# Six diffusion layers: attention outputs in four tiles of 32 columns, and values only for the heads that a half of the partitions keeps

## The chip, the cores and the metric

The kernel runs on one core of a Trainium2 chip. Its time is the device time of one execution in microseconds (us). A profiled execution gives the span, from the first to the last recorded instruction, and the duration of every instruction on every engine: TensorE (PE, with its weight loads listed apart as PEld), VectorE (DVE), ScalarE (ACT), GpSimd (POOL) and the DMA queue of SyncE (SP).

## What is computed

The program is a chain of eight residual blocks on x of 16 batches x 64 tokens x 128 features: a recurrent decoder, a mixture of experts, a latent attention, a quantised feed-forward, then the block of this case, then another mixture, an attention block and a last mixture. The block of this case has six layers, each with 16 heads of 8 features:

```python
for i in range(NL):                                   # NL = 6
    xn = _adaln(x, noise_emb, n1_w[i], n1_b[i])
    q, k, v = jnp.split(xn @ qkv_w[i].T, 3, axis=-1)
    q, k = _rope(q), _rope(k)
    x = x + _attn(q, k, v, src_mask).reshape(B, L, D) @ so_w[i].T
    xn = _adaln(x, noise_emb, n2_w[i], n2_b[i])
    q, k, v = _rope(xn @ cq_w[i].T), _rope(context @ ck_w[i].T), context @ cv_w[i].T
    x = x + _attn(q, k, v, ctx_mask).reshape(B, L, D) @ co_w[i].T
    xn = _adaln(x, noise_emb, n3_w[i], n3_b[i])
    x = x + gelu(xn @ f1_w[i].T + f1_b[i]) @ f2_w[i].T + f2_b[i]
```

`_attn` is a masked softmax over 64 keys; `_adaln` is a layer norm with a scale and a shift per batch; `_rope` is a rotary embedding. All arithmetic is in fp32.

## The kernel before

The six layers are written by `layers` (L2087). Every layer works on two halves of the batches, h = 0 and 1, of 8 batches (512 tokens) each, and in each half it does self attention ("s"), cross attention ("c") and a feed-forward. The keys and values of cross attention depend only on the context and are computed for a whole layer at its head.

The order of the work is not written by hand. Every step is put down with `plan.op(engine, ns, emit, deps, takes, ...)`: the engine it runs on, an assumed duration in ns, what it depends on, and the kind of buffer that it takes. `_Plan.order` (L1183) then goes through the steps greedily: of all steps that are ready, the one that could start first goes next, and of those that could start together the one with the longest remaining path. The instructions of each engine are emitted in that order, and each engine keeps it. So an assumed duration has no effect on what an instruction costs, but it sets the order of all instructions of the stage. `_Plan.fills` (L1234) adds small bf16 matmuls (`units`) to the PE queue where the plan leaves PE idle or sees little activity (from each step's `area`); they compute nothing that is used.

Buffers in PSUM are few: two of kind `pj` (one bank each, for projections and transposes), one `S` (four banks, scores) and one `O` (two banks, attention outputs). A step that takes a buffer waits until the one who had it before has been read out.

**One attention of one half** (`attend_half`, L2354). After the norm and two projections for queries (`rotary_half`), `qx` holds queries of which all but 8 of each 32 partitions are zeroed, so that one matmul with 32 rows gives the scores of one head per group of partitions. The partitions of a score tile are 64 keys for each of two heads: the lower 64 partitions belong to one head of a pair, the upper 64 to the other. Then, for each p of four (two batches each):

- `scores`: 16 fp32 matmuls into S (the trace has 32 weight loads and 32 matmuls of it, two for each);
- P = exp(S) by ACT, 128 x 1024 (L2405);
- `outputs`: 16 fp32 matmuls, each with a weight tile of P of 128 partitions x 64 columns (64 queries) and 18 moving columns of V: 16 with the values of a pair of heads, and two that give the softmax's sums.

For two p together, `inv` is the reciprocal of the sums (L2414) and `On` the normalised output (L2418), both on DVE; then a transpose (L2424), a copy by ACT (L2426), the output projection, and the addition to x (L2431).

**Keys and values** (`keys_values`, L2329). V is a tile of 128 partitions x (8 batches, 8 pairs of heads, 18). On the lower 64 partitions only the first head's 8 values of each pair may be non-zero, on the upper 64 only the second's, since both are summed over all partitions. The kernel before computes all 128 value features on both halves of the partitions (two matmuls for each batch, one for each half of the partitions, 128 moving columns), four batches to a `pj` buffer, so two buffers for a half. DVE multiplies by `pk`, the product of the key mask and of `par`, which is zero where a partition's half does not keep the head:

```python
nc.vector.tensor_tensor(V[:, g * 4:(g + 1) * 4, :, 0:16], t.slot[1]...,
    pk.unsqueeze(2).to_broadcast([128, 4, 8, 16]), ALU.mult)
```

Every value of V is thus written anew for every layer, except columns 16 and 17 of each pair, which are set once by two POOL instructions for each of the six V tiles (L2130; one tile for each half of self attention, two for each half of cross attention).

The decoder, at the start of the program, uses another tiling of TensorE in `mm4` (L1334): a product with 128 output partitions is cut into four matmuls of 32 weight columns. Its steps `su` and `cb` have 16 and 2 moving columns. It is not touched by the change.

Of the kernel before, what the change touches and what calls it, by code (L numbers as in the profile page):

```python
# [14 lines left out]
ALU = mybir.AluOpType  # L15
# [3 lines left out]
B, T, D = 16, 64, 128  # L19
# [1269 lines left out]
class _Fast(_Net):  # L1289
# [797 lines left out]
    def layers(self):  # L2087
        nc, tc = self.nc, self.tc
        x0 = self.x
        out = self.new_x()  # L2090
        with ExitStack() as st:
            pool = st.enter_context(tc.tile_pool(name="l_sb", bufs=1))
            ps = st.enter_context(tc.tile_pool(name="l_ps", bufs=1, space=PSUM))
            plan = _Plan()

            buffers = self.plan_buffers(plan, pool)
            buffers("pj", 2, [128, 512], where=ps)
            buffers("S", 1, [128, 4, 512], where=ps)
            buffers("O", 1, [128, 2, 512], where=ps)
            at = self.at["l"]  # L2100
            for (kind, a, b), n in zip(self.LPARTS, (2, 1, 1, 2, 1)):
                buffers(kind, n, [128, at[b][1] - at[a][0]], True)
            for kind, n, shape in (
                *self.NORM, ("xT", 3, [128, 512]), ("u", 3, [128, 2, 512]), ("qr", 2, [128, 512]),
                ("qx", 2, [128, 2048]), ("On", 4, [128, 2, D]), ("oT", 4, [128, 256]),
                ("ada", 2, [128, 6, B]),
                ("P", 8, [128, 1024]),
            ):
                buffers(kind, n, shape, kind == "ada")
            self.plan, self.inv = plan, self.tile(pool, [128, NL, 2, 2, 64], "inv")  # L2110


            self.keep = []
            for k, n in (("s", 1), ("c", 2)):
                u8 = pool.tile([128, B], U8, tag="u8" + k, name="u8" + k)
                nc.sync.dma_start(out=u8, in_=self.ins["km_" + k])
                m8 = self.tile(pool, [128, B], "m8" + k)
                nc.vector.tensor_copy(m8, u8)
                nc.vector.tensor_scalar(m8, m8, -1.0, 1.0, ALU.mult, ALU.add)
                pk = self.tile(pool, [128, B, 16], "pk" + k)  # L2120
                nc.vector.tensor_tensor(
                    pk, self.c("par").unsqueeze(1).to_broadcast([128, B, 16]),
                    m8.unsqueeze(2).to_broadcast([128, B, 16]), ALU.mult)
                self.keep.append(pk)
                for h in range(2):
                    buffers(f"kr{k}{h}", n, [128, 512], True)
                    vs = [self.tile(pool, [128, 8, 8, 18], f"V{k}{h}{v}") for v in range(n)]
                    for V in vs:
                        for c in range(2):
                            nc.gpsimd.tensor_tensor(  # L2130
                                V[:, :, :, 16 + c], self.c("par2")[:, c:c + 1].unsqueeze(1).to_broadcast([128, 8, 8]),
                                m8[:, h * 8:(h + 1) * 8].unsqueeze(2).to_broadcast([128, 8, 8]), ALU.mult)
                    plan.buffers(f"V{k}{h}", vs, True)
            ctxT = self.tile(pool, [128, NTOK], "ctxT")

            def context(h):
                t = plan.op("PE", 900, lambda t: [nc.tensor.transpose(
                    t[:, k * 128:(k + 1) * 128], self.ctx[:, h * 4 + k, :], self.ident) for k in range(4)], (), "pj", area=427)
                return plan.op("ACT", 600, lambda _: nc.scalar.copy(ctxT[:, h * 512:(h + 1) * 512], t.slot[1]), [t])

            cs = [context(h) for h in range(2)]
            xs = [out[:, h * 4:(h + 1) * 4, :] for h in range(2)]

            qs = [[self.quarter_norm(x0[:, h * 4:(h + 1) * 4, :], k, None, True, xs[h]) for k in range(2)]
                  for h in range(2)]
            tops = [[o for _, o in qs[h]] for h in range(2)]
            for n in range(NL):
                w = self.layer_loads(n)
                kv = [self.keys_values(w, "c", cs[h], lambda h=h: ctxT[:, h * 512:(h + 1) * 512], h) for h in range(2)]
                ada = self.layer_adapt(w)  # L2150
                for h in range(2):
                    tops[h] = self.attend_half(w, "s", n, h, xs[h], ada, None, tops[h],
                                               [q for q, _ in qs[h]] if n == 0 else None)
                for h in range(2):
                    tops[h] = self.attend_half(w, "c", n, h, xs[h], ada, kv[h], tops[h])
                for h in range(2):
                    tops[h] = self.ffn_half(w, h, xs[h], ada, tops[h], x0 if n == NL - 1 else None)
            with tc.manual_schedule(engines=None):
                plan.run(fill=self.fill, banks=("pj", "S", "O"))
            self.watch(0, self.inv.rearrange("p n k h t -> p (n k h t)"))  # L2160
        self.x = out
# [167 lines left out]
    def keys_values(self, w, kind, dep, src, h):  # L2329


        nc, plan = self.nc, self.plan
        c = "" if kind == "s" else "c"
        V = plan.op("SP", 0, lambda _: None, takes=f"V{kind}{h}")
        kr = self.rotary_half(w, (c + "k", c + "ks"), src, dep, f"kr{kind}{h}", [V])
        load, wv = w(c + "v")
        Vs = []
        for g in range(2):

            def values(t, g=g):  # L2340
                for k in range(4):
                    bt = (g * 4 + k) * T
                    keys = src()[:, bt:bt + T]
                    for r in (slice(0, 64), slice(64, 128)):
                        self.mm(t[r, k * 128:(k + 1) * 128], keys, wv())

            t = plan.op("PE", 1050, values, [load, dep], "pj", peers=[V])
            pk = self.keep["sc".index(kind)][:, h * 8 + g * 4:h * 8 + g * 4 + 4, :]
            Vs.append(plan.op("DVE", 690, lambda V, g=g, t=t, pk=pk: nc.vector.tensor_tensor(
                V[:, g * 4:(g + 1) * 4, :, 0:16], t.slot[1].rearrange("p (b c v) -> p b c v", b=4, c=8),  # L2350
                pk.unsqueeze(2).to_broadcast([128, 4, 8, 16]), ALU.mult), [t], on=V))
        return kr, Vs

    def attend_half(self, w, kind, n, h, x, ada, kv, top, ns=None):  # L2354

        nc, plan = self.nc, self.plan
        i = "sc".index(kind)
        c = "" if kind == "s" else "c"
        xT = self.adaln_half(x, ada, i, h, top, ns)
        src = lambda: xT[0].home.slot[1]  # L2360
        qr = self.rotary_half(w, (c + "q", c + "qs"), src, xT, "qr")
        kr, Vs = self.keys_values(w, kind, xT, src, h) if kv is None else kv
# [3 lines left out]
        def copy(t, j):  # L2366
# [5 lines left out]
            else:  # L2372
# [3 lines left out]
        qxs = [plan.op("ACT" if j == 3 else "DVE", 730 if j == 3 else 450, lambda t, j=j: copy(t, j), [qr], on=qx,  # L2376
                       peers=[qx]) for j in (3, 0, 1, 2)]
        O = plan.op("SP", 0, lambda _: None, [kr] + qxs, "O")

        def scores(S, p):  # L2380
            for bb in range(2):
                b = 2 * p + bb
                tok = slice(b * T, (b + 1) * T)
                for h2 in range(2):
                    for g in range(4):
                        rows = slice(32 * g, 32 * g + 32)
                        at = (b * 2 + h2) * 128
                        self.mm(S[h2 * 64:(h2 + 1) * 64, g, bb * 128:(bb + 1) * 128],
                                kr.slot[1][rows, tok], qx.slot[1][rows, at:at + 128])

        def outputs(O, p, P):
            Pv = P.slot[1].rearrange("p (g b q t) -> p g b q t", g=4, b=2, q=2)
            for g in range(4):
                for q in range(2):
                    for bb in range(2):
                        hp = 2 * g + q
                        at = (p % 2) * 144 + hp * 18
                        self.mm(O[bb * 64:(bb + 1) * 64, p // 2, at:at + 18], Pv[:, g, bb, q, :],
                                Vs[0].home.slot[1][:, 2 * p + bb, hp, :])

        load, wo = w(c + "o")
        os, adds = [], []
        for p in range(4):
            S = plan.op("PE", 950, lambda S, p=p: scores(S, p), [kr] + qxs, "S", peers=[O], area=427)
            P = plan.op("ACT", 1030, lambda P, S=S: nc.scalar.activation(  # L2405
                P.rearrange("p (g c) -> p g c", g=4), S.slot[1][:, :, 0:256], AF.Exp,
                scale=1.0 / math.sqrt(8.0)), [S], "P", table="exp")
            os.append(plan.op("PE", 950, lambda O, p=p, P=P: outputs(O, p, P), [P, *Vs], on=O, area=240))
            if p % 2 == 0:
                continue  # L2410
            k = p // 2
# [122 lines left out]
```

## Time and profile before

| | |
|---|---|
| three runs | 1675.52, 1684.32, 1690.44 us; median 1684.32 |
| the profiled execution | 1676.6 us, of which the span is 1672.9 |
| stage of the six layers | about 603 to 1176 us of the span |
| one layer in the middle | 797.8 to 890.0 us: 92.2 us |
| PE busy in that layer | 81.0 us; DVE 60.2, ACT 34.9, POOL 21.6 |
| O matmuls in that layer | 512 matmul records in 16 steps, 17.4 us busy |
| value matmuls in that layer | 128 records in 8 groups of 16, 8.4 us busy |
| scores in that layer | 512 records in 16 steps; P by ACT 16 x 1020 ns |
| granted PE clock in that layer | 1.00 |

A matmul's record is longer than the distance to the next one, since matmuls overlap: 32 records of about 212 ns stand within 1.1 us. The price of a step of many matmuls is therefore taken from the start of its first record to the start of what follows it on PE.

### The profile page before, as it was taken

To read this page: it belongs to the slowest core of one execution; us is meant where nothing else is said; L and a number is where in the kernel's file an instruction comes from. 1 tells how busy PE (TensorE), PEld (TensorE's weight loads), DVE (VectorE), ACT (ScalarE), POOL (GpSimd) and SP (SyncE) were. 2 spreads that over 40 slices of the span, in tenths; PEclk is the share of its full clock that TensorE was granted. 3 is DMA by queue.
4 is the path that set the end of the run, shared out by engine and by line. 5 is a ranking of instruction groups with operands and counts; after the bars stand their busy time and mean duration, and the time that the engine had idled before them with its cause. 6 is when DMAs were issued, how large, how long until landed. Compare 5 with 4: busy or idle time off the path is not lost.

```text
span 1672.9 us, 47624 instructions
## 1 busy us (share of the span) xinstructions
PE 1501.6 (90%) x21466; PEld 1092.4 (65%) x21466; DVE 783.3 (47%) x2505; ACT 536.1 (32%) x885; POOL 185.5 (11%) x227
## 2 busy tenths in 40 slices
PE   6999989999997599998898888888999899999997
PEld 5888856666777246666565656655576677776665
DVE  4435351226334656556676667565311544445112
ACT  2111134432331213424343333434433233332431
POOL 0000010002000032222222122122000101001000
PEclk7555579999999769989999999999999999999999
DMA  6000000000000041000000000000300200000000
GB/s 223 4 5 4 4 2 1 0 1 2 1 2 10 0 175 30 7 25 18 29 17 20 13 20 12 7 16 2 140 2 1 102 2 2 3 2 1 1 1 15
DMA packets 14338, 38.48 MB, mean 23 GB/s; under 512 B 1682, under 2 KB 6674, under 8 KB 14125
## 3 DMA queue, kind: packets, MB, share of 16 engines
q1 hardware_dynamic: 14125, 35.34, 6.2%
q8 instruction: 170, 2.79, 0.7%
q14 instruction: 43, 0.35, 0.1%
HBM read 34.81 MB, written 0.52 MB: 21 GB/s over the span
## 4 chain that ended last, share of the span: by engine, by line
PE 82%; DVE 12%; ACT 3%; issue 2%; DMA 1%; SPq 0%; POOL 0%; ACTq 0%; DVEq 0%
PE pj L296 41%; PE y L296 11%; PE O L296 9%; PE S L296 6%; PE cb L296 3%; PE hh L296 3%; PE lg L296 3%; DVE qx L2373 2%; DVE u L2323 1%; PE pj L1928 1%; ACT P L2451 1%; PE su L296 1%; PE pj L2264 1%; ACT bd L1568 1%; DVE nq L2211 1%
## 5 line engine op out<-in xcount | busy, mean ns | idle before, releaser
L296 PEld LDWEIGHTS y<-m_sb,H 128*128 128x128 f32 x1568 | 188.6, 192 | 57.3 <-issue 35.6
L296 PE MATMUL y<-m_sb,H 128*128 128x128 f32 x1568 | 193.5, 276 | 16.8 <-DVE x L1732 9.8
L296 PE MATMUL pj<-xT,m_sb 128*128 128x512 f32 x392 | 183.8, 598 | 0.0
L2217 POOL TENSOR_TENSOR nq<-nq,minus_half 128x2 f32<-128x2 f32 x120 | 85.2, 715 | 602.1 <-DVE nq L2214 568.5
L2405 ACT ACTIVATE P<-S 128x1024 f32<-128x1024 f32 x96 | 97.9, 1020 | 111.3 <-PE S L296 111.3
L1708 ACT ACTIVATE H<-pj,m_sb 128x512 f32<-128x512 f32 x128 | 87.5, 687 | 132.7 <-PE pj L296 132.4
L1732 DVE SCALAR_TENSOR_TENSOR x<-y,cw,x 128x128 f32<-128x128 f32 x128 | 39.0, 346 | 186.8 <-PE y L296 186.8
L296 PEld LDWEIGHTS pj<-xT,m_sb 128*128 128x128 f32 x392 | 68.9, 191 | 57.4 <-issue 56.9
L2247 ACT ACTIVATE xn<-x,nq 128x128 f32<-128x128 f32 x100 | 48.4, 492 | 152.4 <-DVE nq L2220 142.6
L2323 DVE TENSOR_TENSOR u<-pj,consts_sb 128x512 f32<-128x512 f32 x96 | 66.2, 690 | 35.4 <-PE pj L296 35.0
L1838 DVE COPY QKV<-pj 128x512 f32<-128x512 f32 x56 | 38.7, 691 | 72.5 <-PE pj L296 72.3
L296 PE MATMUL cb<-bd,E 128*32 128x2 f32 x4096 | 65.5, 193 | 3.3 <-issue 3.2
L1708 ACT ACTIVATE H<-pj,b1g,m_sb 128x512 f32<-128x512 f32 x64 | 49.6, 778 | 58.5 <-PE pj L296 55.8
L296 PEld LDWEIGHTS cb<-bd,E 128*32 128x32 f32 x4096 | 62.9, 156 | 3.5 <-issue 3.3
L296 PE MATMUL pj<-xT,w_sb 128*128 128x512 f32 x128 | 63.0, 611 | 1.4 <-DVE xT L2292 1.4
L296 PE MATMUL pj<-xT,l_f 128*128 128x512 f32 x96 | 50.4, 618 | 11.9 <-ACT P L2451 11.8
L1895 ACT ACTIVATE P<-S 128x1024 f32<-128x1024 f32 x32 | 32.8, 1024 | 85.0 <-PE S L296 84.7
L1732 DVE SCALAR_TENSOR_TENSOR acc<-y,cw,acc 128x128 f32<-128x128 f32 x64 | 19.5, 346 | 86.5 <-PE y L296 86.5
L296 PE MATMUL pj<-units 128*128 128x512 bf16 x195 | 55.7, 396 | 4.5 <-DVE x L2079 1.9
L1584 ACT ACTIVATE H<-hh 128x16 f32<-128x16 f32 x64 | 12.9, 202 | 138.8 <-PE hh L296 138.8
L296 PEld LDWEIGHTS O<-QKV,P 64*64 64x64 f32 (+1 forms) x1536 | 48.7, 135 | 13.2 <-issue 5.3
L296 PE MATMUL O<-QKV,P 64*64 64x65 f32 (+1 forms) x1536 | 55.2, 222 | 2.0 <-DVE On L1923 1.8
(363 smaller groups left out, 2738.9 us busy)
## 6 DMA issues: line engine op xcount, KB each, us to landing
w_sb<-in_w SPq DMA_DIRECT2D x7, 681.5 KB, 8.3
m_sb<-in_m SPq DMA_DIRECT2D x8, 515.0 KB, 7.6
m_sb<-in_m SPq DMA_DIRECT2D x8, 514.5 KB, 5.9
m_sb<-in_m SPq DMA_DIRECT2D x7, 565.5 KB, 9.3
l_f<-in_l SPq DMA_DIRECT2D x6, 578.5 KB, 3.9
l_a<-in_l SPq DMA_DIRECT2D x6, 387.0 KB, 3.1
l_s<-in_l SPq DMA_DIRECT2D x6, 384.0 KB, 3.2
w_sb<-in_w SPq DMA_DIRECT2D x4, 512.5 KB, 11.7
```

The lines of the kernel that those rows point to most:

```text
L296: self.nc.tensor.matmul(out, lhsT=lhsT, rhs=rhs, start=start, stop=stop, **kw)
L1568: nc.scalar.activation(bd, lg, AF.Exp)
L1708: nc.scalar.activation(a[:, c, :], ups[c].slot[1], act, bias=b, scale=g)
L1732: nc.vector.scalar_tensor_tensor(acc[:, k, :], src, g, x0[:, i, :] if first else acc[:, k, :], ALU.mult, ALU.add)
L1838: e(o, i.rearrange("p (b t) -> p b t", t=T) if len(o.shape) == 3 else i)
L1895: P = plan.op("ACT", 1030, lambda P, S=S: nc.scalar.activation(P.rearrange("p (j n) -> p j n", j=2), S.slot[1], AF.Exp, scale=0.125), [o f ...
L1928: t = plan.op("PE", 700, lambda t, On=On: [nc.tensor.transpose(t[:, i * 128:(i + 1) * 128], On.slot[1][:, i * 128:(i + 1) * 128], self.ide ...
L2217: return lambda t: nc.gpsimd.tensor_tensor(t[:, :, b], t[:, :, a], self.minus_half[:, 0:2], ALU.pow)
L2247: nc.scalar.activation(o, xk[:, i, :], AF.Identity, bias=f[1], scale=f[0])
L2323: us.append(plan.op("DVE", 690, lambda u, t=t, k=k, table=table: nc.vector.tensor_tensor(view(u[:, k, :]), view(t.slot[1]), self.c(table). ...
L2373: nc.vector.tensor_scalar(o, r, m, None, ALU.mult)
L2405: P = plan.op("ACT", 1030, lambda P, S=S: nc.scalar.activation(P.rearrange("p (g c) -> p g c", g=4), S.slot[1][:, :, 0:256], AF.Exp, scale ...
```

## The change

Three things are changed in the six layers, and nothing else.

1. In `outputs`, each matmul of 64 weight columns becomes two of 32, so that the four tiles of 32 output partitions (two batches x two halves of the 64 queries) are written by four matmuls in turn. The number of matmuls doubles, from 16 to 32 for each p; each still has 18 moving columns.
2. In `keys_values`, a matmul for each half of the partitions has as moving operand only the 8 columns of each pair that this half keeps: 64 moving columns instead of 128. All 8 batches fit in one `pj` buffer. Two DVE steps, of 64 partitions each, write the kept 8 values of each pair into V, times the key mask. The other 8 values are never written by them; they are set to zero once, by a POOL memset for each V tile, which together with the two old POOL instructions is now a step of the plan (`fresh`) that the first writing of the tile waits for.
3. The assumed durations in the plan: values 970 ns once (2 x 1050 before), scores 640 ns (950), outputs 600 ns (950). The `area` of scores and outputs is left as it was.

```diff
-                pk = self.tile(pool, [128, B, 16], "pk" + k)
-                nc.vector.tensor_tensor(
-                    pk, self.c("par").unsqueeze(1).to_broadcast([128, B, 16]),
-                    m8.unsqueeze(2).to_broadcast([128, B, 16]), ALU.mult)
-                self.keep.append(pk)
+                self.keep.append(m8)
...
-                    for V in vs:
+
+                    def fresh(V, h=h, m8=m8):
+                        nc.gpsimd.memset(V, 0.0)
                         for c in range(2):
                             nc.gpsimd.tensor_tensor(
                                 V[:, :, :, 16 + c], self.c("par2")[:, c:c + 1].unsqueeze(1).to_broadcast([128, 8, 8]),
                                 m8[:, h * 8:(h + 1) * 8].unsqueeze(2).to_broadcast([128, 8, 8]), ALU.mult)
+
+                    self.fresh[k, h] = [plan.op("POOL", 1600, lambda _, V=V, f=fresh: f(V)) for V in vs]
...
-        for g in range(2):
-
-            def values(t, g=g):
-                for k in range(4):
-                    bt = (g * 4 + k) * T
-                    keys = src()[:, bt:bt + T]
-                    for r in (slice(0, 64), slice(64, 128)):
-                        self.mm(t[r, k * 128:(k + 1) * 128], keys, wv())
-
-            t = plan.op("PE", 1050, values, [load, dep], "pj", peers=[V])
-            pk = self.keep["sc".index(kind)][:, h * 8 + g * 4:h * 8 + g * 4 + 4, :]
-            Vs.append(plan.op("DVE", 690, lambda V, g=g, t=t, pk=pk: nc.vector.tensor_tensor(
-                V[:, g * 4:(g + 1) * 4, :, 0:16], t.slot[1].rearrange("p (b c v) -> p b c v", b=4, c=8),
-                pk.unsqueeze(2).to_broadcast([128, 4, 8, 16]), ALU.mult), [t], on=V))
-        return kr, Vs
+        def values(t):
+            for b in range(8):
+                for j in range(2):
+                    self.mm(t[j * 64:(j + 1) * 64, b * 64:(b + 1) * 64], src()[:, b * T:(b + 1) * T],
+                            wv().rearrange("p (c j v) -> p j c v", j=2, v=8)[:, j])
+
+        t = plan.op("PE", 970, values, [load, dep], "pj", peers=[V])
+        keep = self.keep["sc".index(kind)][:, h * 8:(h + 1) * 8]
+
+        def place(V, j):
+            r = slice(j * 64, (j + 1) * 64)
+            nc.vector.tensor_tensor(
+                V[r, :, :, j * 8:(j + 1) * 8], t.slot[1][r, :].rearrange("p (b c v) -> p b c v", b=8, c=8),
+                keep[r].unsqueeze(2).unsqueeze(3).to_broadcast([64, 8, 8, 8]), ALU.mult)
+
+        fresh = [fresh.pop(0)] if fresh else []
+        return kr, [plan.op("DVE", 690, lambda V, j=j: place(V, j), [t, *fresh], on=V) for j in range(2)]
...
-                    for bb in range(2):
-                        hp = 2 * g + q
-                        at = (p % 2) * 144 + hp * 18
-                        self.mm(O[bb * 64:(bb + 1) * 64, p // 2, at:at + 18], Pv[:, g, bb, q, :],
+                    hp = 2 * g + q
+                    at = (p % 2) * 144 + hp * 18
+                    for k in range(4):
+                        bb, half = k // 2, slice(k % 2 * 32, k % 2 * 32 + 32)
+                        self.mm(O[k * 32:(k + 1) * 32, p // 2, at:at + 18], Pv[:, g, bb, q, half],
                                 Vs[0].home.slot[1][:, 2 * p + bb, hp, :])
...
-            S = plan.op("PE", 950, lambda S, p=p: scores(S, p), [kr] + qxs, "S", peers=[O], area=427)
+            S = plan.op("PE", 640, lambda S, p=p: scores(S, p), [kr] + qxs, "S", peers=[O], area=427)
...
-            os.append(plan.op("PE", 950, lambda O, p=p, P=P: outputs(O, p, P), [P, *Vs], on=O, area=240))
+            os.append(plan.op("PE", 600, lambda O, p=p, P=P: outputs(O, p, P), [P, *Vs], on=O, area=240))
```

More of the change, by code (lines that the diff above doesn't have):

```diff
@@ L2110, in layers @@
             self.plan, self.inv = plan, self.tile(pool, [128, NL, 2, 2, 64], "inv")
-            self.keep = []
+            self.keep, self.fresh = [], {}
             for k, n in (("s", 1), ("c", 2)):
@@ L2333, in keys_values @@
         c = "" if kind == "s" else "c"
+        fresh = self.fresh[kind, h]
         V = plan.op("SP", 0, lambda _: None, takes=f"V{kind}{h}")
@@ L2336, in keys_values @@
         load, wv = w(c + "v")
-        Vs = []
-        for g in range(2):
-            def values(t, g=g):
-                for k in range(4):
-                    bt = (g * 4 + k) * T
-                    keys = src()[:, bt:bt + T]
-                    for r in (slice(0, 64), slice(64, 128)):
-                        self.mm(t[r, k * 128:(k + 1) * 128], keys, wv())
-            t = plan.op("PE", 1050, values, [load, dep], "pj", peers=[V])
-            pk = self.keep["sc".index(kind)][:, h * 8 + g * 4:h * 8 + g * 4 + 4, :]
-            Vs.append(plan.op("DVE", 690, lambda V, g=g, t=t, pk=pk: nc.vector.tensor_tensor(
-                V[:, g * 4:(g + 1) * 4, :, 0:16], t.slot[1].rearrange("p (b c v) -> p b c v", b=4, c=8),
-                pk.unsqueeze(2).to_broadcast([128, 4, 8, 16]), ALU.mult), [t], on=V))
-        return kr, Vs
+        def values(t):
[12 more added lines that the diff above has]
+        return kr, [plan.op("DVE", 690, lambda V, j=j: place(V, j), [t, *fresh], on=V) for j in range(2)]
     def attend_half(self, w, kind, n, h, x, ada, kv, top, ns=None):
```

## The prediction, made before the changed kernel was run

> **What bounds the kernel now.** I read the page's busy shares first, then the busy time by stretch for one layer, then the chain of waits and PE's timeline in that layer. The whole program is PE-heavy, and so is a layer. The second line is one layer: width, then busy time and count of PE, PEld, DVE, ACT, POOL, then granted clock, DMA share and GB/s.
>
> ```profile
> PE 1501.6 (90%) x21466; PEld 1092.4 (65%) x21466; DVE 783.3 (47%) x2505; ACT 536.1 (32%) x885; POOL 185.5 (11%) x227
> 797.80:890.00 92.20, 80.98 (x1360) 55.95 (x1360) 60.15 (x183) 34.90 (x50) 21.56 (x22) 1.00 0.07 21
> ```
>
> PE is busy 81.0 of 92.2 us, at full clock, with DMA at 7%: neither the clock nor the weights' loading is the limit here. The share alone doesn't tell whether a shorter PE step shortens the layer, so I took the chain of waits in this layer (start, length, what, count):
>
> ```profile
> 831.41 0.89 PE O L296 x32
> 832.31 0.62 PE S L296 x32
> 832.93 2.00 PE O L296 x64
> 834.93 0.02 issue
> 834.95 0.37 DVE inv L2414
> ...
> 840.95 0.62 PE S L296 x32
> 841.57 1.04 PE O L296 x32
> 842.62 0.64 PE pj L296 x4
> 843.26 0.62 PE S L296 x32
> 843.88 1.04 PE O L296 x32
> ```
>
> All 16 output steps of the layer are on that chain, about 1.04 us each, 16.6 us or 18.0% of it. But there are two patterns. In the first half's attention (831.4 to 837.1) outputs follow one another on PE and then DVE waits for them. In the second half's, outputs stand between scores, and S has one buffer: the next scores can't start before P has been read. That loop shows in the waits (total, times, longest):
>
> ```profile
> ACT P L2405 <- PE S L296: 17.0, 13, 2.9
> PEld S L296 <- ACT P L2405: 2.0, 5, 0.8
> ```
>
> Scores start at 838.87, 840.88, 843.19 and 845.23: 2.01, 2.31 and 2.04 us apart. 2.04 us is the loop without anything else in it: 0.69 scores, about 0.1, 1.02 P, 0.17 back, measured where PE's wait before the scores is the 0.17 on P. A shorter output step can only take away the 0.27 us above that.
>
> [...] The trace has 31 (2.00 us for 64), 53 (0.85 us for 16) and 14.5 (0.45 us of loads for 32)[...]. [...]
>
> **1. Outputs.** 16 matmuls of 64 columns become 32 of 32, so 64 pairs of load and matmul instead of 32. [...] The trace has the very form, 128*32 on four tiles, in the decoder, here while the clock was full:
>
> ```profile
> 21.24 0.72 PE L296 MATMUL cb<-bd,E 128*32 128x2 f32 x63
> 832.86 2.05 PE L296 MATMUL O<-Vs,P 128*64 128x18 f32 x64
> 827.28 1.97 PE L296 MATMUL pj<-l_s,xT 128*64 128x128 f32 x32
> ```
>
> Less the last record's own 0.17, 0.55 us for 62 gaps is 8.9 ns. With 2 moving columns that is a lower end; `su`, 16 columns, has about 10 to 11 ns over eight pairs. So 64 pairs take 0.57 to 0.68 us; I take 0.60. At the half clock later in the decoder `cb` has 13.2 ns, the bad end (0.85). A step saves 1.04 - 0.60 = 0.44 us; 96 steps, 42 us of PE time.
>
> **2. Values.** A half has 32 pairs before and after, all with 64 weight columns; only the stream goes from 128 to 64 columns. Before: 2 x 0.90 to 1.0. [...] Saved: 0.5 to 0.9 us, I take 0.7; 24 calls, 17 us of PE time, together 59.
>
> DVE keeps two multiplications of 512 elements for each partition in each call, 0.69 us each by the row before (64 partitions instead of 128 change nothing that the rows show; bounds 0.6 to 0.75). One `pj` buffer is taken instead of two, but held over 1.0 to 1.3 of PE and both multiplications.
>
> **3. What of it is on the path.** Walking the layer 797.8 to 890.0: first half, self: four outputs in a row with DVE waiting behind them, the whole 4 x 0.44 = 1.76 us. Second half, self: 0.27 from the spacing; then the last output, now at 847.71, can't start before its P, which ends at 847.42, plus 0.17: 0.12 earlier and 0.44 shorter; 0.8 together. Cross attention repeats both (862.1 to 869; scores at 870.53, 872.51, 874.82, 876.85): 1.76 and 0.8. Sum 5.1 of 7.0. Of eight value groups in a layer about four stand on the chain (830.3, 839.9, 858.5 and at 819.9 nearly); the others lie where PE waits for DVE's query copies anyway (853.0, with 1.72 us idle after it). I take half, 1.2. So 6.3 us for a layer, 38 for six. The last layer has no next layer's keys to fit in, and fills stand in its gaps: 2 us less. What is late next is the S-P loop, then DVE's `u` and `qx`.
>
> **4. POOL, once.** Six memsets of 1152 elements. Rows of POOL memsets: 206 ns for 128, 112 for 16, so 0.84 ns an element, 1.07 us each, 6.4 in all; the old 12 multiplications (3.5 us) stay. They are now plan steps, ready at time zero, so one comes ahead of the norm's power operations (715 ns each), and its multiplications wait for the mask at 604.3. Behind it on POOL stand the eight powers of both halves, and for these DVE and ACT wait to normalise. Before, `Vc` held five powers back until 608.5 too, and PE waited for weights at 608.95. Cost 0 to 6 us; I take 3. The two `pk` multiplications (0.8 us of DVE) go.
>
> **5. The plan.** The 950 ns for scores was 0.3 too long; 640 and 600 are what I measure or expect. The order of the whole stage changes. That can gain (other work fits in the loop's 1.4 us gap) or lose (a query copy behind a value copy): -10 to +15 us, I take 0. The fills (113 `units` matmuls in the stage, some 0.21 us apart) may grow by a few a layer: 0 to 3 us, in gaps. SP's queue issues no DMA more or less; its weight loads wait for buffers that come free earlier. 3072 more pairs of instructions are fetched; no wait of that kind shows in the layers.
>
> **Sum.** -38 + 2 + 3 = -33. Against the profiled execution, 1676.6 - 33 = 1643.6; that one lies 7.7 under the median of the runs, so **1651**.
>
> **Rivals.**
> - **PE bounds throughout**: the plan fills the loop's gaps, and all 59 us but the 3 at the start come through: 1628. For it: 88% PE share and the queue order on the chain. Against it: 2.04 us in the loop.
> - **The S-P loop takes over**: with shorter outputs the first half's phases go to the loop's pace too, so only 0.8 a phase is left: 4 x 6 x 0.8 = 19, less 3: 1668, down to nothing, 1684. For it: ACT's P waits; against it: P of the first half is ready before its outputs.
> - **The tiles don't overlap as meant**: 13.2 to 14.5 ns a pair makes outputs 0.85 to 0.93, 11 to 18 us, half of values 9: about 1665 to 1675. Against it: 8.9 ns at full clock.
> - **Slower, by the `pj` buffers**: the one value tile waits on DVE for two multiplications, in queue behind the three query copies (2.29 us at 827.38); meanwhile PE has one `pj` for projections that each need 0.69 of DVE. Before, a PE wait of 0.45 for `Vs` stands at 830.32. If a call costs 2.5 us more, 24 x 2.5 - 33 = +27: 1711. It decides from 1.4 us a call. Against it: 24 buffers fewer are taken, and DVE's work is the same.
>
> **Chances.** Forecast 0.47, PE throughout 0.22, loop 0.14, no overlap 0.06, slower 0.11. A measurement can tell about 1% (17 us) from no change. Most of the forecast, all of the second and a little of the third and fourth are faster by that: 0.72; slower 0.11; the rest 0.17. The range 1622 to 1690 takes in the second rival, with a few us of better order, and the loop; it leaves out the slower case and little below.
>
> **What would show it.** Right: output steps of 64 pairs in 0.57 to 0.68 us; value steps of 32 in 0.99 to 1.28; scores of a second half 2.04 apart; layers of 85 to 87 us; POOL 6 to 7 us more, all before 640. Wrong: outputs over 0.85; layers at 83 or less (PE throughout) or over 90; more PE waits on DVE `V` or `u`; stretches of the layers with a clock below 1.00 beyond the few now.

## The result: slower, by 1.4%

| | before | after |
|---|---|---|
| median of four runs, us | 1686.53 (1675.52 to 1690.44) | 1707.19 (1705.70 to 1709.90) |
| profiled execution / its span, us | 1676.6 / 1672.9 | 1708.1 / 1704.6 |
| first transposes of the layers to the last `f2` matmul, us | 573.6 | 604.2 |
| PE busy in that stretch, us | 508.0 | 491.9 |
| granted PE clock, whole span / that stretch | 0.914 / 0.98 | 0.905 / 0.95 |

The changed kernel takes 1.0139 times as long (95%: 1.0107 to 1.0171). The span grew by 31.7 us and the stage of the layers by 30.6, so nearly everything happened there. And it happened although PE was *busy 16.1 us less* in the stage.

In the page after, the shares of busy time and the instruction queue's line (packets, MB, share of the DMA engines) read:

```profile
PE 1486.1 (87%) x24590; PEld 1056.1 (62%) x24590; DVE 784.2 (46%) x2503; ACT 534.5 (31%) x885; POOL 189.5 (11%) x233
q8 instruction: 194, 3.18, 0.8%
```

PE is busy for less time, with 3124 more matmul records; the other engines do what they did. The layer that corresponds to the one shown before, in the view of busy time by stretch:

```profile
811.85:911.46 99.61, 82.57 (x1883) 52.24 (x1883) 60.34 (x183) 34.68 (x50) 21.20 (x23) 0.93 0.08 21
```

It is 7.4 us longer, with 523 more matmuls. This layer ran at a granted clock of 0.93, that of before at 1.00, so its busy times are not to be set against those of before. Compare the steps instead. Those that ran undisturbed are as short as was meant; PE's timeline has (start, duration of the records, form, count):

```profile
836.71 1.15 PE L296 MATMUL pj<-l_s,xT 128*64 128x64 f32 x32
837.80 1.12 PE L296 MATMUL pj<-xT,l_s 128*128 128x512 f32 x2
...
858.41 0.74 PE L296 MATMUL O<-Vs,P 128*32 128x18 f32 x64
859.08 0.71 PE L296 MATMUL pj<-l_s,oT 128*128 128x128 f32 x4
```

Read from start to start: values 1.09 us, outputs 0.67 us. So the four tiles do overlap: a matmul every 10.5 ns (0.67 us for 64), where two tiles had one every 32.5 before (1.04 us for 32). But the chain of waits through the same layer shows what happens to the output step next to it:

```profile
849.70 0.62 PE S L296 x32
850.32 0.55 PE O L296 x43
850.87 1.45 issue
852.32 0.31 PE O L296 x13
...
863.66 0.46 PE O L296 x33
864.12 1.50 issue
865.61 0.44 PE O L296 x31
```

A step of 64 matmuls is **cut in two** by 1.45 or 1.50 us in which PE waits for nothing that the profile shows: no semaphore, no buffer, no other engine. (The chain leaves out records that ran beside the step before; PE's timeline has 51 and 13 of them, and 33 and 31: all 64.) Before, no output step had such a gap. After, PE stands 36 times in output steps, 39.6 us together, measured from the start of one weight load to the next; two of these, 1.2 us, are waits for P. It also stands eight times inside a scores step, 5.2 us, and seven times between two matmuls into `pj`, 6.1 us. (Six more gaps of 1.6 us lie between two scores steps. There PE waits for P, and o64 and half below have them too.) In the view of waits for this layer (total, times, longest) it appears as

```profile
PEld O L296 <- issue: 9.6, 17, 1.8
PE O L296 <- issue: 7.1, 6, 1.7
```

**What PE waits for.** The trace's packet records show when the instruction queue moves a block. Every block has 16,384 bytes. There were 170 before and 194 after; 24 more blocks for the 6144 loads and matmuls that the change adds is 64 bytes an instruction, 256 instructions a block. PE has 49,323 records after, which fill 193 such blocks, so this queue carries PE's instructions. Of 35 stalls over 0.4 us inside output steps, 33 end 1.1 to 1.6 us after a block's packet has ended. Five of them:

```
block ended   PE stands            resumes after the block's end
850.83        850.66 to 852.32     1.49
860.15        860.59 to 861.59     1.44
864.25        863.90 to 865.61     1.36
887.45        886.97 to 888.90     1.45
899.88        899.89 to 901.32     1.44
```

The place of the stalls says the same. Number PE's records (loads, matmuls and the few of its sequencer) in order of their start: of the 36 stalls over 0.2 us in output steps, 34 end at a record whose number leaves the remainder 193 on division by 256. The other two are the waits for P. So PE always stops at the same place of a block, where one ends and the next begins, whichever matmul it happens to be at.

Two blocks never start closer than 3.11 us in this trace, nor closer than 3.24 in that of before. If that is the limit, PE gets at most 256 / 3.11 = 82 instructions for each us over a longer stretch (an estimate). Over no 20 us of the stage does this trace have more than 79 for each us, or that of before more than 57. In the loop of scores and P (843.19 to 845.23 before, 2.04 us) the kernel before issues 64 instructions for scores, 64 for outputs and 4 for a transpose: 132, or 65 for each us. With 128 for outputs it is 196, or 96 for each us. A step at full pace asks for 128 in 0.67 us, and in the first half several follow one another. Over the whole layer it is only 38 for each us: it is the bursts that run dry.

**A second place: POOL, once.** POOL's timeline where the layers begin, after:

```profile
602.74 1.06 POOL L2126 MEMSET Vs<- 128x1152 f32 x1 [24.76 <-PE pj L340]
612.77 0.55 POOL L2128 TENSOR_TENSOR Vs<-consts_sb,m8s 128x64 f32<-128x64 f32 x2 [8.97 <-issue]
613.27 5.29 POOL L2217 TENSOR_TENSOR nq<-nq,minus_half 128x2 f32<-128x2 f32 x8
```

and before:

```profile
603.18 1.41 POOL L2217 TENSOR_TENSOR nq<-nq,minus_half 128x2 f32<-128x2 f32 x2 [26.37 <-DVE nq L2211]
...
608.53 3.29 POOL L2217 TENSOR_TENSOR nq<-nq,minus_half 128x2 f32<-128x2 f32 x5
```

The first multiplication waits 8.97 us, "issue" again, with its mask there since 605.4. The trace's records have an instruction MODIFY_POOL_CONFIG ahead of POOL's first multiplication of this stage; I call it the program change. Before, it stands at 576.8 us, in idle time. After, a memset comes first, with no such instruction ahead of it (602.74), and the change stands behind it at 603.82, with the eight powers of the norms behind it: they end at 618.6 instead of 611.8. From this instruction to the first multiplication 8.95 us pass (603.82 to 612.77), 7.3 of them after the mask is there.

### The profile page after: what moved, and what is told of

It reads as the page before. It is cut to its first block, busy times and chain, and to the rows that moved or that the text cites. A ratio compares the mean times of both kernels' runs of the same rounds, so it can differ in the third digit from the quotient of the medians.

```text
span 1704.6 us, 53906 instructions
## 1 busy us (share of the span) xinstructions
PE 1486.1 (87%) x24590; PEld 1056.1 (62%) x24590; DVE 784.2 (46%) x2503; ACT 534.5 (31%) x885; POOL 189.5 (11%) x233
## 4 chain that ended last, share of the span: by engine, by line
PE 76%; DVE 14%; issue 5%; ACT 4%; DMA 1%; POOL 0%; SPq 0%; ACTq 0%; DVEq 0%
PE pj L296 39%; PE y L296 11%; PE O L296 7%; PE S L296 6%; PE cb L296 3%; PE hh L296 3%; PE lg L296 3%; ACT P L2410 2%; DVE u L2323 2%; PE pj L1928 1%; PE su L296 1%; DVE qx L2377 1%; DVE nq L2211 1%; DVE xT L2289 1%; DVE xn L2245 1%
## 5 line engine op out<-in xcount | busy, mean ns | idle before, releaser
L296 PE MATMUL pj<-units 128*128 128x512 bf16 x238 | 65.5, 395 | 4.2 <-DVE x L2079 1.9
L2419 DVE RECIPROCAL inv<-O 128x32 f32<-128x32 f32 x48 | 17.1, 357 | 92.4 <-PE O L296 92.2
L2264 PE MATMUL pj<-consts_sb,xn 128*128 128x128 f32 x184 | 41.8, 312 | 19.7 <-ACT xn L2247 10.9
```

Of the source, the lines that this page charges most:

```text
L296: self.nc.tensor.matmul(out, lhsT=lhsT, rhs=rhs, start=start, stop=stop, **kw)
L2264: self.nc.tensor.transpose(t[:, at:at + 128], n[0].slot[1][:, i, :], self.ident)
L2419: r = plan.op("DVE", 380, lambda _, Ov=Ov, inv=inv: nc.vector.reciprocal(inv, Ov()[:, :, :, 16:18]), os[p - 1:])
```

## The experiments

My theory after the result was: PE runs out of fetched instructions. Its rivals: the planner's new order, or a fault of the four tiles themselves. Ratios are to the kernel before, run beside each.

**1. o64**: all of the change, but outputs in two tiles of 64 columns, the plan's 600 ns kept, so that the order stays.

```diff
-                    for k in range(4):
-                        bb, half = k // 2, slice(k % 2 * 32, k % 2 * 32 + 32)
-                        self.mm(O[k * 32:(k + 1) * 32, p // 2, at:at + 18], Pv[:, g, bb, q, half], ...
+                    for bb in range(2):
+                        self.mm(O[bb * 64:(bb + 1) * 64, p // 2, at:at + 18], Pv[:, g, bb, q, :], ...
```

> The changed kernel with the outputs alone put back to 64 columns (64 instead of 128 PE instructions a step; assumed durations kept, so the order of all steps is the same). Theory fetch (PE runs out of instructions, since a step of 128 is over before the next block of instructions has come): the 36 stalls inside output steps, 39.6 us, go to under 5 us; the 96 steps get 0.35 us longer each, 33 us, of which part is hidden; the time falls to 1685 to 1700. Theory order (the new order of the steps and the loop of scores and P cost the time): nothing is won, the longer steps add 10 to 35 us: 1717 to 1740.

1689.79 us, 1.0034 (1.0011 to 1.0056). The stage's blocks go from 89 to 65, and no output step has a stall over 0.4 us. One layer:

```profile
802.90:895.10 92.20, 82.18 (x1374) 54.44 (x1373) 60.16 (x183) 34.71 (x50) 21.18 (x23) 0.98 0.08 21
```

The *longer* output step makes this layer 7.4 us shorter, and the stage 20.7 (583.5 against 604.2), with the same order. The theory of fetching held.

**2. half**: four tiles of 32 columns as in the change, but two pairs of heads share a matmul, so half as many; every second pair of heads is computed with the other pair's softmax weights.

```diff
-                for q in range(2):
-                    hp = 2 * g + q
-                    at = (p % 2) * 144 + hp * 18
+                at = (p % 2) * 144 + g * 36
...
-                        self.mm(O[k * 32:(k + 1) * 32, p // 2, at:at + 18], Pv[:, g, bb, q, half], ...
+                    self.mm(O[k * 32:(k + 1) * 32, p // 2, at:at + 36], Pv[:, g, bb, 0, half], ...
```

> The changed kernel with half of the output matmuls: one of the two pairs of heads of a group gives the weights for both, with 36 moving columns instead of 18, so every output is written but those of every second pair of heads are computed with the wrong softmax weights. Order and assumed durations are the same; an output step has 64 instructions as before the change, and the tiles are still 32 columns. Theory fetch: stalls inside output steps under 5 us, steps of about 0.4 us, layers of 86 to 90 us, 1640 to 1665. Theory order: PE is 25 us less busy, but the waits stay; layers over 92, 1690 to 1707.

1649.53 us, 0.9782 (0.973 to 0.9833). PE's timeline and the same layer's stretch:

```profile
832.20 0.47 PE L296 MATMUL O<-Vs,P 128*32 128x36 f32 x32
832.60 0.44 PE L2264 MATMUL pj<-consts_sb,xn 128*128 128x128 f32 x2
833.51 0.70 PE L296 MATMUL S<-qx,krs 32*64 32x128 f32 x32 [0.47 <-ACT P L2408]
```
```profile
787.50:874.30 86.80, 74.02 (x1372) 44.78 (x1372) 59.62 (x183) 34.41 (x50) 21.17 (x23) 0.96 0.08 23
```

Same form, half the instructions: 65 blocks in the stage, four stalls over 0.4 us in output steps and none of them 1.1 to 1.6 us after a block. PE now waits for P, the loop that was expected to come next, and this layer takes 86.8 us, as the prediction had it for the change. So the four tiles aren't at fault. This kernel's output step is shorter than that of the change (0.40 against 0.67), so its 57.7 us against the changed kernel aren't the price of fetching alone.

**3. lib_early**: the change, with POOL's program changed in idle time by one tiny multiplication.

```diff
+            early = self.tile(pool, [128, 1], "early")
+            nc.gpsimd.tensor_tensor(early, self.minus_half[:, 0:1], self.minus_half[:, 0:1], ALU.mult)
             self.keep, self.fresh = [], {}
```

> The changed kernel with one small POOL multiplication put ahead of the stage, so that POOL's change of its program (its configuration instruction before the first multiplication after the all-reduce) happens while POOL is idle, as before the change. Theory: the 8.97 us that POOL stood after the first memset go, and 7 to 9 us of the whole: 1698 to 1701. If the start is hidden behind the loads of weights instead: under 2 us, 1705 or more.

1694.59 us, 1.0058 (1.0039 to 1.0076): 12.6 us less than the change, more than expected. POOL's timeline:

```profile
601.25 0.19 POOL L2114 TENSOR_TENSOR early<-minus_half 128x1 f32<-128x1 f32 x1 [24.79 <-PE pj L340]
601.58 1.06 POOL L2128 MEMSET Vs<- 128x1152 f32 x1
604.04 0.56 POOL L2130 TENSOR_TENSOR Vs<-consts_sb,m8s 128x64 f32<-128x64 f32 x2 [1.40 <-DVE nq L2215]
604.55 5.29 POOL L2219 TENSOR_TENSOR nq<-nq,minus_half 128x2 f32<-128x2 f32 x8
```

The memset still runs first, at the same 1.06 us, but the powers begin 8.7 us earlier. The memsets were cheap; the program change that they displaced was not.

**4. before_o32**: the kernel before with the outputs block of the change and nothing else.

> The kernel before with the outputs alone in four tiles of 32 columns (order, values and POOL's start as before). Theory fetch: stalls of 25 to 45 us inside output steps eat up the 33 to 40 us of PE time that the steps save: 1670 to 1695, against 1684. Theory order: the order is the old one, so the saving comes through: 1645 to 1665.

1706.91 us, 1.0128 (1.0076 to 1.0181), worse than either theory expected. 32 stalls over 0.4 us, 36.9 us together, all of them after a block and all at the same place of a block. The four tiles alone cost 22.7 us in the old order with the old values: the theory of the order falls.

**5. values_o64** is o64 with the early multiplication and 1000 ns assumed for outputs; **6. values_o64_old_costs** differs by the assumed 950 ns for scores and outputs.

```diff
-            S = plan.op("PE", 640, lambda S, p=p: scores(S, p), [kr] + qxs, "S", peers=[O], area=427)
+            S = plan.op("PE", 950, lambda S, p=p: scores(S, p), [kr] + qxs, "S", peers=[O], area=427)
```

> The changed kernel with outputs of 64 columns, assumed at 1000 ns, scores at 640, the new values, and POOL's configuration early: what of the change has no price in instructions. Theory fetch with values partly on the path: no stalls in output steps; 64-column run less 12 us for the early configuration, less 0 to 8 for an order that knows the steps' true lengths: 1668 to 1680. Theory that the values were hidden behind DVE all along: 1680 to 1690, no faster than before.

> The same with the old assumed durations of scores and outputs (950 both). If the order matters (theory order), this differs from the run with 640 and 1000 by over 8 us; if instructions alone decide (theory fetch), by less than 8.

1679.37 us, 0.9961 (0.9943 to 0.9978), and 1681.66 us, 0.9983 (0.9968 to 0.9998). The order is worth 2.3 us here, and the two intervals overlap. The first of these beats both kernels with the arithmetic unchanged, by 4.5 us over the kernel before.

**7. o32_old_costs**: lib_early with 950 ns for scores and outputs.

> The changed kernel with 32-column outputs, the new values, POOL's configuration early and the old assumed durations of scores and outputs (950 both), against the run with the early configuration alone (1694.6). Theory fetch: stalls inside output steps stay at 30 to 45 us, time within 10 us of 1694.6. Theory order: the old order brings the saving back, under 1670.

1700.92 us, 1.0092 (1.0066 to 1.0118), 6.3 us over lib_early, with stalls of 42.1 us (35.3 there). The old order doesn't help.

**8. o32_bf16**: lib_early with P (for outputs) and V in bf16, which lowers the precision; for the 32 products of a step the records have 64 loads and 64 matmuls in fp32, and 32 of each in bf16. **9. o64_bf16**: the same with two tiles of 64 columns. (The bf16 P has four buffers of its own, and outputs are assumed at 400 and 500 ns.)

```diff
-                    vs = [self.tile(pool, [128, 8, 8, 18], f"V{k}{h}{v}") for v in range(n)]
+                    vs = [pool.tile([128, 8, 8, 18], BF16, tag=f"V{k}{h}{v}", name=f"V{k}{h}{v}") for v in range(n)]
...
-                scale=1.0 / math.sqrt(8.0)), [S], "P", table="exp")
+                scale=1.0 / math.sqrt(8.0)), [S], "Pb", table="exp")
```

> The changed kernel with P and V stored in bf16, so that an output matmul is one load and one matmul instead of two each: all 32 matmuls of 32 columns are there, in 64 instructions, at a lower precision of the outputs; POOL's configuration early, outputs assumed at 400 ns, four buffers for P. Theory fetch: stalls inside output steps under 6 us, 1625 to 1650. Theory that the 32-column tiles themselves cost the time (mode changes, banks, order): no better than 1680.

> P and V in bf16 as in the 32-column bf16 run (1641.2), but outputs of 64 columns: 16 matmuls, 32 instructions a step, at a lower precision of the outputs; assumed at 500 ns. If the four tiles are worth their PE time once instructions are few, steps take 0.5 instead of 0.33 us and the time is 5 to 15 us longer, 1646 to 1656. If the gain of that run was only that of fewer instructions and a shorter step of any kind, it is the same within 4 us, 1637 to 1645.

1641.21 us, 0.9735 (0.9708 to 0.9763), and 1646.42 us, 0.9755 (0.9718 to 0.9792). In o32_bf16 there is no stall over 0.4 us in any output step:

```profile
832.71 0.37 PE L296 MATMUL O<-Vs,Pb 128*32 128x18 bf16 x32
833.02 0.44 PE L2432 MATMUL pj<-consts_sb,On 128*128 128x128 f32 x2
```

The four tiles at the fp32 kernel's old count of instructions are free of stalls. But they then win only about 5 us over two tiles, at the lower edge of what was expected; beside their own runs of before it is under 3, and the two intervals overlap. So a gain of the tiles without stalls isn't clear of noise here. A likely reason, not tested, is that outputs this short no longer set the end.

**10. o32_first_half**: lib_early with 32 columns only in the first half's attention, 64 in the second.

```diff
-                    for k in range(4):
-                        bb, half = k // 2, slice(k % 2 * 32, k % 2 * 32 + 32)
+                    m = 32 if h == 0 else 64
+                    for k in range(128 // m):
+                        bb, part = k * m // 64, slice(k * m % 64, k * m % 64 + m)
```

> All in fp32: four tiles of 32 columns only for the first half's attention (where outputs follow one another on PE), 64 columns for the second half's (where they wait for the loop of scores and P); new values, POOL's configuration early, assumed 600 and 1000. Theory fetch: half of the stalls, 12 to 22 us, against half of the PE saving; between the run with 64 columns throughout (1679.4) and that with 32 (1694.6), or a little under the first where first-half steps stand apart: 1672 to 1690. If a saved PE step were worth its full length there, 1665 or less.

1690.85 us, 1.0031 (1.0007 to 1.0055). Half the steps, half the stalls: 19 of them over 0.4 us, 19.7 us together. It lies between values_o64 and lib_early, just over the expected range, so also where the order leaves room in the chain, the tiles don't pay.

**11. o64_padded** and **12. o64_padded_end** add to each output step of values_o64 16 matmuls of one column that nobody reads, to get the instruction count of the change without its tiles: interleaved, or at the step's end. The second's edit:

```diff
+            for g in range(4):
+                for k in range(4):
+                    self.mm(O[k * 32:(k + 1) * 32, p // 2, 300 + g:301 + g],
+                            Pv[:, g, k // 2, k % 2, 0:32], Vs[0].home.slot[1][:, 2 * p + k // 2, 2 * g + k % 2, 0:1])
```

> The 64-column kernel with early configuration (1679.4) with 16 more matmuls of one moving column in each output step, into unused columns: 128 PE instructions a step as in the changed kernel, but the outputs in two tiles of 64 columns. Theory fetch (the number of instructions alone): stalls come back inside output steps, 15 to 45 us, although the tiles are the old ones; 1705 to 1750. Theory tiles: the steps get 0.3 to 0.4 us longer (29 to 38 us of PE time, part of it hidden), no stalls over 5 us, 1685 to 1710.

> The padded kernel again with the 16 one-column matmuls put together at the end of each output step, so that the tiles change form once in a step and not 16 times (2049.4 with 16). 128 PE instructions a step, outputs in two tiles of 64 columns. Theory fetch: output steps without a stall take 1.3 to 1.5 us, stalls of 15 to 45 us come back inside output steps; 1710 to 1750. Theory tiles: no stalls over 5 us; 1690 to 1715.

2049.40 us, 1.217 (1.2114 to 1.2226), and 1764.73 us, 1.0481 (1.0413 to 1.055). Their output steps, from start to start:

```profile
811.26 4.39 PE L296 MATMUL O<-Vs,P 128*64 128x18 f32 x64
815.58 1.22 PE L296 MATMUL pj<-l_s,oT 128*128 128x128 f32 x4
```
```profile
858.20 1.48 PE L296 MATMUL O<-Vs,P 128*64 128x18 f32 x64
859.61 0.44 PE L2266 MATMUL pj<-consts_sb,xn 128*128 128x128 f32 x2
```

The first says nothing on fetching: its step changes from 64 to 32 columns and back eight times, that of the second once, and takes 4.32 us instead of 1.41: an estimated 0.2 us for each of the 14 further changes (2.91 / 14). The second has the 128 instructions of the change in 1.41 us instead of 0.67, and only four stalls over 0.4 us in its output steps, 2.4 us in all, each after a block. Neither theory's numbers held. That fits a limit on the *rate*, not on the count. It isn't a clean test, though, since its clock was lower (0.88), and only about 96 x 0.4 = 38 us of its 85 over values_o64 is accounted for by longer steps.

## Why the prediction was wrong

1651 us was forecast, 1622 to 1690 with its range; the kernel lies above both, and became slower instead of faster. The terms of the sum against what was measured between pairs of runs:

| part | predicted, us | measured, us | from |
|---|---|---|---|
| values, with order and early program change | -7 | -4.5 | values_o64 against before |
| outputs in four tiles | -31 (5.1 x 6), +2 | +15.2 | lib_early against values_o64, whose plans also differ (600 and 1000 ns for outputs); the tiles alone, after against o64: +17.4 |
| POOL's start | +3 (0 to 6) | +12.6 | after against lib_early |
| sum | -33 | +23.3 | |

The last row compares with 1683.9; beside its own runs of before, the changed kernel is 20.7 us slower.

**The step that failed** is the one costed at nothing: "3072 more pairs of instructions are fetched; no wait of that kind shows in the layers." The observation was true and the conclusion wrong. An absent wait shows that a resource isn't short *yet*, not how much of it is left. A bound could have been looked for in the trace of before: there no two blocks start closer than 3.24 us, at most an estimated 79 instructions for each us (256 / 3.24), while the loop with the change asks for 196 in 2.04 us, 96 for each. In the layers of before, four blocks already followed the one ahead of them by under 4 us; after the change it is 47.

**PE's prices were right.** Outputs took 0.67 us (0.57 to 0.68), values 1.09 (0.99 to 1.28). In the trace of before the distances from one pair of load and matmul to the next are 31 ns in outputs, 53 in values and 14.5 in scores, the last being the upper price of the third rival. The 0.99 us is 32 of the 31 ns, since values have the same 64 weight columns; the 1.28 was an estimate of mine that no trace showed. 96 output steps of 0.67 instead of 1.04 us are 35.5 us less. But PE stands some 50 us at the ends of blocks (38.4 in outputs, 5.2 in scores, 6.1 in `pj`), which is more: by this estimate 14 us are lost, against 17.4 measured between o64 and the change. PE's busy time in the stage fell by no more than 16.1 us, since 52 more fills take 13.8 us of it and the clock was lower. The decoder's 63 matmuls at 8.9 ns proved the tiles' speed and could not show the limit: those are 126 instructions in 0.55 us, under half a block, while the layers ask for it again and again.

**The values step** was worth about what was foretold. One `pj` buffer with two multiplications behind it caused nothing like the 2.5 us a call of the slower rival: that rival had the right sign by luck, with a mechanism that no run shows. A multiplication on 64 partitions took 0.69 us (`Vs`, 64x512), one on 128 before 0.68.

**POOL.** The memsets took 1.06 us as worked out and stood ahead of the eight powers as said. The term was mis-sized because a new first instruction also moved the program change. POOL's busy time grew by 4.0 us, not 6 to 7; the cost was idle time, where no share of busy time shows it.

**The loop of scores and P.** In the layer shown above, the scores of the second half follow one another after 2.34, 2.16 and 2.66 us in self attention rather than 2.04, the last with a 0.80 us stall in it. In cross attention, where no step of the loop was cut, it is 1.94, 2.26 and 1.94. Counted from `f2` to `f2`, five layers of the changed kernel take 92.7 to 99.6 us, all over the 90 that was named as a sign of a wrong forecast. Relieved of instructions, half does run into the P wait; five of its layers take 84.3 to 90.5 us, all but the last under 87. The mechanism of the gain was right for a kernel that doesn't run dry.

**The plan** was taken at 0: the two pairs with old and new costs differ by 2.3 and 6.3 us, in favour of the new ones. **Fills** grew by 52 in the stage (113 to 165), more than "a few a layer", and by the same 52 in o64, which has the same order.

## What to carry to other kernels

Before cutting matmuls into smaller tiles, count the instructions that the busiest stretch issues for each us, and measure how close its instruction blocks lie: here the changed kernel got no more than 79 PE instructions for each us over any 20 us of the layers, and a step that was 0.4 us shorter but had twice as many lost. Look at the densest stretch, not at the mean. Cut PE's instructions (a lower precision, 1641.21 us in o32_bf16; wider moving operands, 1649.53 us in half) before cutting its time. And when an engine's first instruction of a stage changes, see what else happened at the old one.

## What was not expected of the hardware

- **Instruction supply.** Blocks of 256 instructions never came closer than 3.11 us in the changed kernel and 3.24 in the kernel before, and after a stall PE resumed typically 1.4 us behind a block's end. That the supply is the cause rests on the blocks' times, on the one place of a block at which PE stops, on half and on o32_bf16. What sets the rate wasn't tried. In the changed kernel's stage a block's packet starts about 1.1 us (median) after PE has begun the block before it, and takes 1.06 us (median); with the 1.4 us at the end that makes some 3.5 us, which would be the time of a block (an estimate) if only one is fetched ahead.
- **POOL's program change** took 8.95 us, and 12.6 us of the whole time; a multiplication of one column (0.19 us) placed earlier hides it.
- **Changing the matmul's form** between 64 and 32 columns costs an estimated 0.2 us each, from (4.32 - 1.41) / 14, o64_padded against o64_padded_end, whose mean clocks were 0.80 and 0.88.
- **The clock** of the layer shown was 0.93 after the change, against 1.00 before; in the whole stage 0.95 against 0.98. Whether the many small matmuls lower it wasn't settled. It is not what makes the changed kernel slower than before: half had 0.96 in its stage, and was 34.7 us faster than before.
